# Ranks from block totals, and the ranked pass joined with its neighbours, in a stack of graph layers on one core

## The chip, the cores and the metric

The kernel runs on one core of a Trainium2 chip, with one launch. The metric is device time in microseconds (us). The core has five engines with queues of their own: PE multiplies matrices into PSUM, DVE and ACT do elementwise work and empty PSUM, POOL (GpSimd) does small elementwise work and can issue DMAs, and SP here only issues DMAs. Each engine takes its instructions in the order of the program, and waits on semaphores for what another engine or a DMA has to finish first.

## The reference

A graph with 3327 nodes and 64 features goes through four layers. Each layer normalises x, takes relu, sends it through the dense adjacency matrix and adds the result to x. There are eight products with the matrix, called hops 0 to 7 here: two gated (GRU) hops, one ranked hop, three hops with the squared matrix (weights times mask, both the matrix itself), and two hops of the last layer.

```
h = relu(layernorm(x));  x = x + gru_stack(h, adj)              # hops 0, 1: m = adj @ (x @ W), gates
h = relu(layernorm(x));  support = h @ weight                   # hop 2, the ranked one
mask = (adj != 0); rank = cumsum(mask, axis=1); deg = rank[:, -1:]
k = minimum(deg, 100); pos = rank - (deg - k)
w = mask * where(pos > 0, 0.5 ** (k - pos), 0);  x = x + w @ support + bias
h = relu(layernorm(x));  three times: h = (adj * adj) @ h, h = h @ W.T + b   # hops 3, 4, 5
h = relu(layernorm(x));  two times: h = tanh(concat(adj @ h, h) @ W[k])      # hops 6, 7
```

In the ranked hop the weight of a neighbour is 0.5 to the power of the number of nonzero entries that come after it in the row, where that number is below 100. About 0.5% of the entries are nonzero, and every node is its own neighbour.

## The kernel before

**Tiles.** The nodes are padded to 2 x 13 blocks of 128. The kernel reads the transposed matrix: a source block q (26 of them) is 128 partitions, the target nodes are columns. The targets are cut into four chunks c (`CH`: three of 2 x 384 columns, the last of 2 x 512), and the chunks into two groups: group 0 is chunks 0 and 1, group 1 is chunks 2 and 3. A *tile* is one source block against one group: 768 KB for group 0, 896 KB for group 1, loaded by one DMA from SP into one of 19 slots (`Tile.load`, L281). A *unit* is one hop k, one chunk c and one tile: `propagate` (L376) adds it to the chunk's sum in PSUM, with two halves of 64 output partitions side by side. After its 26 units a chunk's sum is finished, and a task (`after[k]`) makes the next features y[k+1][c] from it: for hops 0 and 1 a GRU cell (`gru`, L527), for hop 1 also a layer norm (L497, with one power on POOL, L510), a row added on POOL (L524) and a split of y into three bf16 terms (`in_three`, L563), since the ranked hop multiplies in bf16.

**Order.** A list `units` is written out by hand: `alone(g, k, ...)` is one hop of one group, and `joint(g, k, ...)` is hops k and k+1 of one group on one load of its tiles. In `joint`, the tiles of the other group's sources come first, each used for hop k and, `LATER` tiles later, for hop k+1; then the tiles of the group's own sources for hop k, then the tiles still waiting, and then the own tiles again for hop k+1, which need hop k's result. `sweep` is the number of last tiles that are taken chunk by chunk, so that the first chunk's task runs beside the second chunk's units. `run` (L450) walks the list: `prepare` loads and masks or squares a tile some units ahead, `expand` makes the operand two units ahead, and `spend` lets the tasks advance step by step as estimated PE time passes. A task whose result is needed at once is finished on the spot (`finish`), so its remaining instructions stand directly before the unit that needs it. The order of instructions on each engine is the order of these calls.

```
    alone(0, 2, descending, sweep=0)
    alone(1, 2, descending, sweep=0)
```

**The ranked hop.** It runs alone for each group, in descending order of source block. `prepare` makes a mask of the tile in half a slot on DVE (L331). `expand` (L338) keeps a running count in PSUM over the whole pass, in two pairs of banks: for each tile it adds `rest` times the mask of the tile before, and `tri` times its own mask (the helper `mm`, L173), so that each entry holds the number of nonzero entries behind it, with its own entry marked. ACT turns the counts into bf16 weights (L365), by writing the exponent bits as int16. Because the counts run on through the pass, the tiles have one fixed order, and PSUM's second half is handed from four `temp` banks to two `pair` tiles for its length (`exchange`, `counting`).

**Other places.** Hops 3 to 5 square the tile, in place where both hops of a `joint` are squared, or into `w4` buffers (`square`, L317: two of three on ACT, one on DVE). Constants are made on POOL and DVE in `more_constants` (L127) while the first tiles load.

Of the kernel before, what the change touches and what calls it, by code (L numbers as in the profile page):

```python
# [37 lines left out]

N, D = 3327, 64
# [13 lines left out]
CAP = 100.0  # L53

# [9 lines left out]
KIND = [PLAIN, PLAIN, RANKED, SQUARED, SQUARED, SQUARED, PLAIN, PLAIN]  # L64
NBUF = 19
PREPARE = {PLAIN: 8, RANKED: 16, SQUARED: 8}
EXPAND = 2
LATER = 4
# [12 lines left out]
def kernel(  # L81
# [13 lines left out]
    work = ctx.enter_context(tc.tile_pool(name="work", bufs=6))  # L95
# [26 lines left out]
    rest = const.tile([P, P], BF16, name="rest")  # L122
    tri = const.tile([P, P], BF16, name="tri")
    bitsb = const.tile([P, 1], F32, name="bitsb")
    bsum = const.tile([P, 2, 2], F32, name="bsum")

    def more_constants():  # L127
# [3 lines left out]
        ones = work.tile([P, P], BF16, name="t2")  # L131
        nc.gpsimd.memset(ones, 1.0)

        nc.gpsimd.affine_select(out=tri, in_=ones, pattern=[[-1, P]], compare_op=ALU.is_gt, fill=0.0,
                                base=0, channel_multiplier=1)
        nc.gpsimd.affine_select(out=tri, in_=tri, pattern=[[-1, P]], compare_op=ALU.not_equal, fill=-128.0,
                                base=0, channel_multiplier=1)
        nc.gpsimd.tensor_tensor(rest, ones, tri, ALU.subtract)
        nc.gpsimd.memset(bitsb, (CAP - 128.0) * TWO7)
# [33 lines left out]
    def mm(out, lhsT, rhs, start=True, stop=True, unchecked=False):  # L173

        for h in range(2):
            hs = slice(h * D, (h + 1) * D)
            nc.tensor.matmul(out[hs], lhsT[:, hs], rhs, start=start, stop=stop, skip_group_check=unchecked)  # L179

# [3 lines left out]
    sum_banks = [psum.tile([P, CWM], F32, name=f"sum{i}") for i in range(4)]  # L184
    counting = []

    def second_half(names, shape):
        pool = tc.tile_pool(name=names, bufs=1, space=bass.MemoryType.PSUM, reuse_waits="tile")
        p = pool.__enter__()
        return pool, [p.tile(shape, F32, name=f"{names}{i}") for i in range(2 if len(shape) > 2 else 4)]  # L190

    half = [second_half("temp", [P, CWM])]

    def exchange(names, shape):
        half[0][0].__exit__(None, None, None)
        half[0] = second_half(names, shape)

    def bank(i):
        return sum_banks[i] if i < 4 else half[0][1][i - 4]

    def take(sums=False):

        pool = idle_sums if sums or counting else idle_temps
        for c in list(tasks):
            if not pool and c not in running:
                advance(c)
        i = pool.popleft()
        return i, bank(i)
# [8 lines left out]
    def features(c):  # L217
        return feat.tile([P, width(c)], F32, name=f"hT{c}")
# [33 lines left out]

    def spend(us):

        for c in list(tasks):
            if c in tasks and c not in running:
                tasks[c][1] -= us
                if tasks[c][1] <= 0:
                    advance(c)
# [8 lines left out]
    class Tile:  # L268

        def __init__(self, q, g, in_place):  # L270
# [3 lines left out]
            self.slot = self.mask = self.before = None  # L274
# [48 lines left out]
    newest = {}  # L323

    def prepare(k, c, t):

        if t.slot is None:
            t.load()
        if KIND[k] == RANKED and t.mask is None:
            t.mask, t.before = Mask(t.w), newest.get(t.g)  # L330
            nc.vector.tensor_scalar(t.mask.view, t.view(), 0.0, None, op0=ALU.not_equal)  # L331
            t.used()
            newest[t.g] = t.mask
        if KIND[k] == SQUARED and t.in_place and c not in t.squares:
            t.squares.add(c)
            square(t.view(c), t.view(c), t.q + c)

    def expand(k, c, t):  # L338

        w = width(c)  # L340
        if KIND[k] == PLAIN or t.in_place:
            return t.view(c)
        wide = work.tile([P, 2, CWM], I16 if KIND[k] == RANKED else F32, name="w4", bufs=4)[:, :, :w]
        if KIND[k] == SQUARED:
            square(wide, t.view(c), t.q + c)
            return wide

        if not counting:
            while len(idle_temps) < 4:
                advance(next(iter(tasks)))
            counting.append(True)
            exchange("pair", [P, 2, CWM])
        a, b = GROUPS[t.g]
        pair = half[0][1][c == b]
        for s in range(2):  # L360
            if t.before is not None:
                mm(pair[:, s, :w], rest, t.before.view[:, s, t.cols(c)], start=False, unchecked=True)
            mm(pair[:, s, :w], tri, t.mask.view[:, s, t.cols(c)], start=t.before is None, unchecked=True)
        spend(STREAM_US * w / CWM)
        nc.scalar.activation(wide, pair[:, :, :w], AF.Relu, bias=bitsb, scale=-TWO7)  # L365
        if c == b:
            if t.before is not None:
                t.before.free()
            if t.q == 0:
                t.mask.free()  # L370
                if t.g == 1:
                    counting.clear()
                    exchange("temp", [P, CWM])
        return wide.bitcast(BF16)

    def propagate(k, c, t, rhs, first, last):  # L376
        w = width(c)
        s, b = divmod(t.q, NB)
        cs = chunk_of(b)
        if y[k][cs] is None:  # L380
            finish(cs)
# [3 lines left out]
        terms = y[k][cs] if KIND[k] == RANKED else [y[k][cs]]  # L385
        for n, yk in enumerate(terms):
            yq = yk[:, b - CH[cs][0], s, :]
            for h in range(2):
                nc.tensor.matmul(acc[h * D:(h + 1) * D, :w], yq, rhs[:, h, :], start=first and n == 0,  # L389
                                 stop=last and n == len(terms) - 1)  # L390
        if KIND[k] != RANKED:
            t.used()
        spend(STREAM_US * w / CWM * (0.75 if KIND[k] == RANKED else 1.0))
        if last:
            begin(c, after[k](c, sums.pop((k, c))))
            if KIND[k] == RANKED and (t.g, c) == (1, NC - 1):
                dead.extend(parts.values())
# [3 lines left out]
    def put(k, c, t):  # L401
        units.append((k, c, t))
        if KIND[k] != RANKED or c == GROUPS[t.g][0]:
            t.uses += 1

    def alone(g, k, order, sweep):
        tiles = [Tile(q, g, KIND[k] == SQUARED) for q in order]
        for t in tiles[:NQ - sweep]:
            for c in GROUPS[g]:
                put(k, c, t)  # L410
        for c in GROUPS[g]:
            for t in tiles[NQ - sweep:]:
                put(k, c, t)

    def joint(g, k, sweep):
        a, b = GROUPS[g]
        in_place = KIND[k] == KIND[k + 1] == SQUARED
        waiting = deque()

        def second():  # L420
            t = waiting.popleft()
            for c in (a, b):
                put(k + 1, c, t)

        for q in sources_of(*GROUPS[1 - g]):
            t = Tile(q, g, in_place)
            for c in (a, b):
                put(k, c, t)
            waiting.append(t)
            if len(waiting) > LATER:  # L430
                second()
        own = [[Tile(q, g, in_place) for q in sources_of(c)] for c in (a, b)]
        both = own[0] + own[1]
        for t in both[:-sweep]:
            for c in (a, b):
                put(k, c, t)
        for c in (a, b):
            for t in both[-sweep:]:
                put(k, c, t)
        while waiting:  # L440
            second()
# [3 lines left out]
        for c in (a, b):  # L445
            for t in own[1]:
                put(k + 1, c, t)

    def run():
        count = {}  # L450
        prepared, expanded = 0, deque()
# [282 lines left out]
```

## Time and profile before

| | us |
|---|---|
| three runs, median (lowest to highest) | 753.68 (751.81 to 754.01) |
| the profiled execution | 751.8 |
| its span | 750.1 |
| PE, ACT, DVE, POOL busy | 717.0, 250.6, 235.7, 42.0 |
| DMA from device memory | 243.64 MB, 326 GB/s over the span |
| PE's clock in all slices | full |

The profile has a page with busy times, with the span in 40 slices (each digit is a busy share in tenths), with the groups of instructions, and with the chain of waits that ended last. The chain is followed back from the last instruction: at each step to what released it. A group's row gives the busy time of its engine, the mean time of one instruction in ns, and the idle time ahead of it with what ended it. Matmuls overlap, so the mean time of one is longer than the time from one to the next.

### The profile page before, as it was taken

The numbers are of one execution on the slowest core, as the hardware profiler recorded it, in microseconds if no ns is written. First come the engines' busy times: TensorE is split into PE (matmuls) and PEld (weight loads), VectorE is DVE, ScalarE is ACT, GpSimd is POOL, SyncE is SP. The second block draws the span as 40 slices with busy tenths as digits, with TensorE's granted clock in tenths as the row PEclk, the third lists the DMA queues.
The fourth block names the chain that finished last, engine by engine and source line by source line (L and its number), as shares of the span: only waits on it lengthen the run. The fifth ranks groups of instructions, "written<-read, shape, count | busy, mean of one in ns | idle before, by whom it ended". The sixth has DMA issues, their size and how long they took to land.

```text
span 750.1 us, 12253 instructions
## 1 busy us (share of the span) xinstructions
PE 717.0 (96%) x5240; PEld 345.7 (46%) x5240; DVE 235.7 (31%) x346; ACT 250.6 (33%) x314; POOL 42.0 (6%) x38
## 2 busy tenths in 40 slices
PE   3978999999998999999999999999999999999997
PEld 2423433434456666666334444334444454344444
DVE  6101201326369347431944213430252610000000
ACT  1101001111046777778947422740054501000000
POOL 5100000001102003000300000000020000000000
PEclk9999999999999999999999999999999999999999
DMA  9999994679999999995999949972999299906991
GB/s 294 401 401 406 405 405 187 240 266 404 401 402 400 404 405 384 386 370 201 407 401 400 403 144 398 405 291 77 379 361 313 74 369 405 366 28 229 398 403 68
DMA packets 79174, 245.29 MB, mean 327 GB/s; under 512 B 4880, under 2 KB 5520, under 8 KB 79120
## 3 DMA queue, kind: packets, MB, share of 16 engines
q1 hardware_dynamic: 78240, 243.55, 85.1%
q10 hardware_dynamic: 880, 0.96, 0.5%
q8 instruction: 41, 0.67, 0.4%
q14 instruction: 13, 0.11, 0.0%
HBM read 243.64 MB, written 0.85 MB: 326 GB/s over the span
## 4 chain that ended last, share of the span: by engine, by line
PE 83%; DMA 8%; DVE 5%; SPq 1%; issue 1%; POOL 1%; ACT 1%; ACTq 0%; DVEq 0%; POOLq 0%
PE sum L389 66%; PE pair L179 9%; PE temp L179 8%; DMA adj<-in_adjT 7%; SPq L284 1%; PE sum L179 1%; DMA brow<-in_bias_rows 1%; DVE adj L331 1%; POOL st L510 1%; DVE t L504 1%; DVE st L502 0%; DVE xs L518 0%; DVE adj L321 0%; DVE st L508 0%; DVE t L507 0%
## 5 line engine op out<-in xcount | busy, mean ns | idle before, releaser
L389 PE MATMUL sum<-adj,y 128*64 128x384 f32 (+1 forms) x2704 | 489.8, 516 | 21.7 <-DMA adj<-in_adjT 19.7
L389 PEld LDWEIGHTS sum<-adj,y 128*64 128x64 f32 x2704 | 192.4, 137 | 289.9 <-issue 249.1
L365 ACT ACTIVATE w<-pair,bitsb 128x768 int16<-128x768 f32 x104 | 98.8, 954 | 33.1 <-PE pair L179 30.1
L319 ACT ACTIVATE adj<-adj 128x768 f32<-128x768 f32 (+1 forms) x103 | 86.1, 906 | 30.8 <-DMA adj<-in_adjT 28.6
L467 DVE COPY t<-sum 128x384 f32<-128x384 f32 x16 | 8.9, 558 | 275.0 <-PE sum L389 275.0
L389 PE MATMUL sum<-w,adj 128*64 128x384 bf16 (+1 forms) x624 | 72.9, 340 | 3.4 <-ACT adj L575 2.2
L179 PE MATMUL pair<-adj,tri 128*64 128x384 bf16 (+1 forms) x416 | 70.8, 339 | 0.0
L179 PE MATMUL pair<-adj,rest 128*64 128x384 bf16 (+1 forms) x400 | 68.7, 339 | 0.6 <-ACT w L365 0.4
L331 DVE TENSOR_SCALAR adj<-adj 128x1536 bf16<-128x1536 f32 (+1 forms) x52 | 53.1, 1028 | 51.2 <-PE pair L179 38.6
L321 DVE TENSOR_TENSOR adj<-adj 128x768 f32<-128x768 f32 (+1 forms) x53 | 53.9, 1063 | 46.8 <-DMA adj<-in_adjT 46.8
L510 POOL TENSOR_TENSOR st<-st,mhalf 128x6 f32<-128x6 f32 (+1 forms) x16 | 27.4, 1752 | 560.9 <-DVE st L509 560.9
L538 ACT ACTIVATE w<-temp,bsum 128x384 f32<-128x384 f32 (+1 forms) x14 | 8.6, 611 | 138.8 <-PE temp L179 138.8
L389 PEld LDWEIGHTS <-adj 128*64 128x64 bf16 x624 | 36.8, 110 | 22.0 <-ACT adj L575 2.8
L389 PE MATMUL sum<-w,y 128*64 128x384 f32 x208 | 36.4, 487 | 0.8 <-DVE w L321 0.8
L319 ACT ACTIVATE w<-adj 128x768 f32<-128x768 f32 x35 | 27.5, 838 | 16.0 <-PE sum L389 9.5
L465 ACT COPY t<-sum 128x384 f32<-128x384 f32 (+1 forms) x16 | 8.5, 532 | 71.9 <-PE sum L389 71.9
L179 PEld LDWEIGHTS <-tri 128*64 128x64 bf16 x416 | 24.6, 110 | 12.5 <-issue 1.1
L179 PEld LDWEIGHTS <-rest 128*64 128x64 bf16 x400 | 24.0, 110 | 13.1 <-issue 1.6
L493 ACT COPY hT<-temp 128x384 f32<-128x384 f32 (+1 forms) x12 | 6.1, 506 | 62.7 <-PE temp L179 62.7
L179 PE MATMUL temp<-bd,t 128*64 128x128 f32 (+1 forms) x296 | 24.3, 279 | 0.4 <-ACT t L465 0.4
L321 DVE TENSOR_TENSOR w<-adj 128x768 f32<-128x768 f32 x17 | 16.0, 956 | 25.9 <-PE sum L389 19.7
L389 PEld LDWEIGHTS sum<-w,y 128*64 128x64 f32 x208 | 14.5, 137 | 18.7 <-issue 14.8
(74 smaller groups left out, 273.0 us busy)
## 6 DMA issues: line engine op xcount, KB each, us to landing
adj<-in_adjT SPq DMA_DIRECT2D x156, 768.0 KB, 11.9
adj<-in_adjT SPq DMA_DIRECT2D x130, 896.0 KB, 9.7
adj<-in_weights SPq DMA_DIRECT2D x2, 352.0 KB, 7.1
xs<-in_x SPq DMA_DIRECT2D x1, 640.0 KB, 5.0
out<-xs ACTq DMA_DIRECT2D x3, 192.0 KB, 1.9
out<-xs ACTq DMA_DIRECT2D x1, 256.0 KB, 6.0
xs<-in_x SPq DMA_DIRECT2D x1, 192.0 KB, 2.4
brow<-in_bias_rows ACTq DMA_DIRECT2D x1, 96.0 KB, 6.9
```

Source lines behind the costliest of these rows:

```text
L179: nc.tensor.matmul(out[hs], lhsT[:, hs], rhs, start=start, stop=stop, skip_group_check=unchecked)
L284: nc.sync.dma_start(out=slots[self.slot][:, :, :self.w], in_=adjT[self.q * P:(self.q + 1) * P, :].rearrange("p (s w) -> p s w", s=2)[:, :, ...
L319: nc.scalar.activation(sq, v, AF.Square)
L321: nc.vector.tensor_tensor(sq, v, v, ALU.mult)
L331: nc.vector.tensor_scalar(t.mask.view, t.view(), 0.0, None, op0=ALU.not_equal)
L365: nc.scalar.activation(wide, pair[:, :, :w], AF.Relu, bias=bitsb, scale=-TWO7)
L389: nc.tensor.matmul(acc[h * D:(h + 1) * D, :w], yq, rhs[:, h, :], start=first and n == 0, stop=last and n == len(terms) - 1)
L465: nc.scalar.copy(m, acc[1][:, :width(c)])
L467: nc.vector.tensor_copy(m, acc[1][:, :width(c)])
L504: nc.vector.tensor_tensor(xc[:, :n], v, st[:, 1, :n, None].to_broadcast([P, n, D]), ALU.subtract)
L510: nc.gpsimd.tensor_tensor(st[:, 3, :n], st[:, 2, :n], mhalf[:, :n], ALU.pow)
L538: nc.scalar.activation(gate, ps[:, :w], AF.Sigmoid, bias=bsum[:, cell, g:g + 1])
```

## The change

The counts behind each tile no longer come from a running sum in the ranked hop. They are taken in hop 0, where the same tiles pass anyway. For every tile a mask is made there too (unit kind `COUNT`), and four short matmuls with a block of ones and zeros (`behind`) add its column sums to the totals of all source blocks that come before it. When hop 0 of a group is done, `totals` holds, for each source block and column, the number of nonzero entries in all blocks behind it.

In the ranked hop a tile's mask gets only 127 rows from DVE. The last row is filled from `totals`, by two DMAs from POOL's queue, and `tri` has a row for it, so one product with `tri` gives the whole count and no tile depends on another. The 26 real last rows (`lastw`) are handled as one more unit per chunk (`SPECIAL`): `mask_last` loads them by two DMAs from SP for each group, and `lasty` collects the matching rows of y[2] by twelve small DMAs from POOL for each chunk, at the end of `in_three`. The count is emptied from four single banks again, one half by ACT and the other by DVE.

As the order is free, the ranked hop is joined: hops 1 and 2 of group 0 share their tiles, and hops 2 and 3 of group 1. In `joint`, waiting tiles are now taken two at a time while the own tiles pass. Loads have a look-ahead of their own (`LOAD`, `RESERVE`). The built program has 234 tile loads instead of 286, 208 `behind` matmuls in place of 400 `rest` matmuls, and 152 DMAs on POOL instead of none.

```diff
-PREPARE = {PLAIN: 8, RANKED: 16, SQUARED: 8}
-LATER = 4
+LOAD = 16
+PREPARE = {COUNT: 6, PLAIN: 6, RANKED: 12, SQUARED: 6}
+RESERVE = 3
...
-        nc.gpsimd.tensor_tensor(rest, ones, tri, ALU.subtract)
+        nc.gpsimd.memset(tri[:, P - 1:P], 0.0)
+        nc.gpsimd.memset(bitsb, BITS)
+        nc.gpsimd.memset(lasty, 0.0)
...
     def prepare(k, c, t):
...
+            rows = P - 1 if kind == RANKED else P
+            nc.vector.tensor_scalar(t.mask.view[:rows], t.view()[:rows], 0.0, None, op0=ALU.not_equal)
             t.used()
-            newest[t.g] = t.mask
+            if kind == RANKED:
+
+                for ch in GROUPS[t.g]:
+                    finish(("count", ch))
+                for s in range(2):
+                    nc.gpsimd.dma_start(out=t.mask.view[P - 1:P, s, :],
+                                        in_=totals[t.g][s * D + t.q:s * D + t.q + 1, :])
...
     def expand(k, c, t):
...
         for s in range(2):
-            if t.before is not None:
-                mm(pair[:, s, :w], rest, t.before.view[:, s, t.cols(c)], start=False, unchecked=True)
-            mm(pair[:, s, :w], tri, t.mask.view[:, s, t.cols(c)], start=t.before is None, unchecked=True)
-        spend(STREAM_US * w / CWM)
-        nc.scalar.activation(wide, pair[:, :, :w], AF.Relu, bias=bitsb, scale=-TWO7)
+            i, ps = take()
+            mm(ps[:, :w], tri, t.mask.view[:, s, t.cols(c)])
+            if s:
+                nc.vector.tensor_scalar(wide[:, s], ps[:, :w], BITS, 0.0, op0=ALU.add, op1=ALU.max)
+            else:
+                nc.scalar.activation(wide[:, s], ps[:, :w], AF.Relu, bias=bitsb)
+            give(i)
...
+    def count(t, first, last):
+        for c in GROUPS[t.g]:
+            w = width(c)
+            if first:
+                counts[c] = take()
+            for s in range(2):
+                nc.tensor.matmul(counts[c][1][s * D:(s + 1) * D, :w], behind[:, NQ - 1 - t.q:NQ - 1 - t.q + D],
+                                 t.mask.view[:, s, t.cols(c)], start=first, stop=last)
...
+    def mask_last(g):
...
+        nc.gpsimd.memset(v, 0.0)
+        rows = adjT.rearrange("(q p) (s n) -> q p s n", p=P, s=2)
+        for s in range(2):
+            nc.sync.dma_start(out=v[s * D:s * D + NQ], in_=rows[:, P - 1, s, w0:w0 + w])
+        yield 12.0
+        nc.vector.tensor_scalar(v, v, 0.0, 129.0 * TWO7, op0=ALU.not_equal, op1=ALU.mult)
...
     def propagate(k, c, t, rhs, first, last):
...
+        if t is SPECIAL:
+            for ch in range(NC):
+                if ch != c:
+                    finish(ch)
+            terms = [[lasty[:, h, i, :] for h in range(2)] for i in range(3)]
+            rhs = [rhs, rhs]
...
     def in_three(h, c):
...
+        yield 1.5
+        b0, b1 = CH[c]
+        for s in range(2):
+            for h in range(2):
+                for i in range(3):
+                    q = h * D + s * NB
+                    nc.gpsimd.dma_start(out=lasty[q + b0:q + b1, h, i, :], in_=terms[i][P - 1:P, :, s, :])
...
-    alone(0, 0, ascending, sweep=2)
-    joint(1, 0, sweep=3)
-    alone(0, 1, ascending, sweep=6)
-    alone(0, 2, descending, sweep=0)
-    alone(1, 2, descending, sweep=0)
-    alone(1, 3, ascending, sweep=6)
-    joint(0, 3, sweep=8)
+    alone(0, 0, sweep=2, lag=5)
+    joint(1, 0, sweep=3, later=4, lag=2)
+    joint(0, 1, sweep=6, later=10)
+    joint(1, 2, sweep=6, later=5)
+    joint(0, 3, sweep=8, later=4)
...
     begin(NC, more_constants())
+    begin(NC + 1, mask_last(0))
+    begin(NC + 2, later_task(60.0, mask_last(1)))
     run()
```

## The prediction

> **What bounds the kernel now.** I read the page first (shares, slices, groups), then the chain of waits in order of time, then the timelines of POOL and SP in the first 36 us.
>
> The page, head, slices and six groups:
>
> ```profile
> PE 717.0 (96%) x5240; PEld 345.7 (46%) x5240; DVE 235.7 (31%) x346; ACT 250.6 (33%) x314; POOL 42.0 (6%) x38
> ...
> DMA  9999994679999999995999949972999299906991
> ...
> L389 PE MATMUL sum<-adj,y 128*64 128x384 f32 (+1 forms) x2704 | 489.8, 516 | 21.7 <-DMA adj<-in_adjT 19.7
> L365 ACT ACTIVATE w<-pair,bitsb 128x768 int16<-128x768 f32 x104 | 98.8, 954 | 33.1 <-PE pair L179 30.1
> L179 PE MATMUL pair<-adj,rest 128*64 128x384 bf16 (+1 forms) x400 | 68.7, 339 | 0.6 <-ACT w L365 0.4
> L331 DVE TENSOR_SCALAR adj<-adj 128x1536 bf16<-128x1536 f32 (+1 forms) x52 | 53.1, 1028 | 51.2 <-PE pair L179 38.6
> L510 POOL TENSOR_TENSOR st<-st,mhalf 128x6 f32<-128x6 f32 (+1 forms) x16 | 27.4, 1752 | 560.9 <-DVE st L509 560.9
> adj<-in_adjT SPq DMA_DIRECT2D x156, 768.0 KB, 11.9
> ```
>
> PE is the bound, and POOL is nearly empty. Durations of matmuls overlap, so rates come from the chain of waits (start, us, what):
>
> ```profile
> 47.43 14.85 DMA adj<-in_adjT
> 62.32 2.16 PE sum L389 x12
> 64.48 3.87 PE temp L179 x24
> ...
> 250.02 0.65 PE pair L179 x8
> ...
> 251.16 0.65 PE pair L179 x8
> ...
> 397.06 41.28 PE sum L389 x256
> ```
>
> A 384-column f32 matmul instruction costs 41.28/256 = 0.161 us (four a unit: 0.645). A ranked unit of 384 columns costs 251.16 - 250.02 = 1.14: eight pair matmuls at 0.081 (0.65) and six rank matmuls (0.49). For 512 columns the chain has 0.86 for eight, 0.107 each. Until 62.3 the end is set by loads: the PE timeline at 54 to 60 us has a tile every 1.95 us with 0.45 us of waiting in it.
>
> POOL and SP at the start (start, us, engine):
>
> ```profile
> 16.23 1.64 POOL L510 TENSOR_TENSOR st<-st,mhalf 128x8 f32<-128x8 f32 x1 [2.20 <-DVE st L509]
> 17.82 0.20 POOL L132 MEMSET t<- 128x128 bf16 x1
> ...
> 20.68 0.20 POOL L141 MEMSET t<- 128x128 f32 x1
> ```
>
> ```profile
> 2.97 34.22 SPq L284 DMA_DIRECT2D adj<-in_adjT  x20
> ```
>
> SP issues the first tile at 2.97; PE gets it at 12.39.
>
> **What the Trainium skill says.** "DMA: Bandwidth & Descriptors", section "Latency and other measured facts": a DMA issued from GpSimd has about 1 us to the first byte, put down to its descriptors being emitted in software; section "Anatomy of one DMA — SWDGE (gpsimd) path" adds a fixed 2 us to completion, and says that DMA engines do not wait on semaphores, the issuing sequencer does. The last agrees with the trace: SP's own waits list 344.6 us for PE. No run here shows a DMA from POOL. "SBUF — State Buffer", section "SBUF: two separate sides": a DVE instruction in a two-port mode keeps GpSimd from writing descriptors. The masks are such instructions by their rate (958 ns for 1536 elements, while the two-input square takes 984 for 768).
>
> **The change, part by part** (against the span, 750.1).
>
> *PE work.* The 400 `rest` matmuls go: 300 x 0.081 + 100 x 0.107 = 35.0. The counts add 208 matmuls, 0.32 us a tile of group 0 and 0.37 of group 1. In the first pass 21 of 26 fit in the 0.45 us of waiting per tile; five follow the last tile (1.6), and group 1 pays 9.8 in full. SPECIAL adds three units of 0.49 and one of 0.65: 2.1. Net -21.5.
>
> *Loads.* 286 tile loads become 234, since hops 1 and 2 of group 0, and 2 and 3 of group 1, share tiles. That pays only where PE waits: PE is idle 12.8 us after 62.3 (windows: 687.7 minus 674.9 busy), at the load-bound hop 1 (chain at 196 to 206), the starts of the ranked passes and at 347 to 368. I take -10.
>
> *The start.* `mask_last(0)` runs before the schedule, so its two small loads stand ahead of all tiles in SP's order, and the first waits for a POOL memset that stands behind all four L510 and the constants. L510 ends at 17.87; the constants without `rest` and with two small memsets end near 20.3; the 128x768 memset is 2.44 (128x2816, L111) x 768/2816 = 0.67. So SP goes on at 21.0, two issues of 0.6, and the first tile is issued at 22.3 instead of 2.97. Behind the waiting instruction stand all tiles, and PE behind them. Some of these 19.3 us come back, since x and weights are long in: I take the shortest landing of a tile in the trace, 4.5 us, instead of the first one's 9.4. First tile at 26.8 instead of 12.4; this stage is paced by loads, so nothing hides it: +14.4.
>
> *The joined order.* In hop 1 with pass 2 of group 0, the last tiles are its own, and the built program's PE order has the first ranked matmul of tile 0 directly behind them. It needs y[2] of chunk 0. From the end of that sum: L467 0.56, gates 3.87, L546, L547, L551 1.78, L553 to L557 2.03, transposes 0.65, L518 0.56, L502 to L509 2.62, L510 1.65, L513 and L514 0.73, in_three 2.13: 16.6, with some 20 hand-overs 18.5. PE meanwhile has the other chunk's six units (3.9), gates 3.9, tri 1.0, transposes 0.7: 9.4. Wait 9. Chunk 1's gates stand behind that; its y[2] costs 4 more. +13. In hop 0 to 1 of group 1 the loop drains the waiting tiles before the end, so the cover is three units and two counts: +2. Before, four waiting tiles (6 us) lay there.
>
> *POOL's queue.* 104 row DMAs (two a mask) and 48 for `lasty` (twelve a chunk), all in POOL's order with L510 and L524. A row also waits until PE has left that half of the slot; behind it waits L510, and DVE's L514 for that. Price unknown in the trace: 0.3 us if generation overlaps, 1.4 if masks lock it out; I take the skill's 1 us, and 2 to complete.
> (a) In that pass PE reaches the first ranked unit at about 22 us (22 units of hop 1 at 0.645, and some 8 of gates). The third mask is wanted four ranked units of 0.81 and two of 0.645 later, at 26.5. Twelve DMAs for chunk 2, possible from about 15 us, go ahead of its rows, which wait for PE at 22, then for the queue at 27: done at 31, wait 4.5. Twelve for chunk 3, gated by DVE's evictions, start at 33; they end at 45, two more rows and completion make 49. PE is there 4.5 after 31, at 35.5: wait 13.5. Sum 18.
> (b) After y[2] of chunk 0 (18.5): L524 1.1, 12 for its `lasty`, 12 rows, and only then chunk 1's L510, at 43.6. y[2] of chunk 1 comes at 48.7 where PE is ready at 32.7: 16 instead of 4. Then its own twelve, to 60.7 and 2; PE reaches SPECIAL at 53.6: 9. Sum 21 over the part above.
> (c) Pass 2 with hop 3 of group 1: 2 us of POOL against 3.4 of PE a tile, except in the rank-only stretch of own tiles: +3.
> Together +42.
>
> *Hidden.* Evictions split between ACT and DVE: per ranked tile of group 0 DVE does 0.96 + 2 x 0.56 = 2.1, PE 1.6 to 2.9. With squares in group 1: 1.10 + 1.25 + 0.73 = 3.1 against 3.4. Covered by PE unless DVE is held up; without cover some 10. Buffers (hT one instead of two, t2 five): readers finish long before, 0.
>
> Sum: -21.5 - 10 + 14.4 + 13 + 2 + 42 = +40, span 790. What lies around it is 751.8 - 750.1 = 1.7. The profiled execution, 751.8, is 1.9 under the median of the three runs (753.68), so 793 beside that; I round down to 790, as PE may get to the lasty bursts with some rows already in.
>
> **Rivals.**
> 1. *POOL is not felt* (0.3 us a DMA or less): -21.5 - 10 + 14.4 + 15 = -2 and nothing for POOL: span 748, time 750 (752 beside the median), 0.3% faster. For: POOL is 94% free; the DMAs are tiny. Against: bursts of twelve stand directly ahead of rows and of L510. It decides below about 0.35 us, where POOL's 42 shrink to some 2.
> 2. *Half price* (0.6 us): (a) 10, (b) 8, (c) 2: 20 in place of 42, so 768.
> 3. *Masks and descriptors block each other, or DVE becomes the bound* of the joined passes (1.4 us a DMA, or the uncovered 10 and more): (a) 29, (b) 35, 42 becoming 69, so 817.
> 4. *The start costs nothing* because SP's wait is met earlier: 776. The POOL order speaks against it.
> That loads drop is certain from the built program.
>
> **How the numbers follow.** Forecast 0.58 (own range 775 to 808), rival 1 0.11, rival 2 0.13, rival 3 0.14, rival 4 0.04. Below 752 lies 0.1, above 822 another 0.08: range 752 to 822. The measurement tells 0.3% from no change. Faster by over that takes most of rival 1: 0.08; within it 0.03; slower 0.89.
>
> **What would show it.** First tile matmul at 26 to 27 us and PE in the first pass ending near 77; a POOL row of 104 and 48 DMA issues near 1 us; waits of PE for POOL's DMAs (tri matmuls on mask rows, SPECIAL on lasty) of 25 to 50 us in hop 1 with pass 2; one L510 late by 10 us or more there; hops 3 to 7 unchanged in length. PE after the first pass short of waits would make the forecast wrong, as would a first tile at 13 us.

## The result: 8.3% slower

| | before | after |
|---|---|---|
| median of the runs (lowest to highest), us | 753.0 (751.81 to 754.01) | 815.71 (813.21 to 818.48) |
| span of the profiled execution, us | 750.1 | 811.4 |
| TensorE's mean clock in it | 1.000 | 0.978 |

The ratio is 1.0834, with a 95% interval of 1.0792 to 1.0876. The forecast was 790 with a range of 752 to 822: the direction and the range held, the likeliest value was 26 us too low. Single terms of its sum were wrong by up to 30 us, in opposite directions.

The page of the kernel after, with the lines that answer to those shown of before:

```profile
PE 721.9 (89%) x5072; PEld 355.5 (44%) x5072; DVE 343.0 (42%) x508; ACT 217.2 (27%) x322; POOL 134.2 (17%) x196
...
PEclk9999999999989969999999999999999999999999
DMA  3899969449127437336647996999167899981992
...
L464 PE MATMUL sum<-adj,y 128*64 128x384 f32 (+1 forms) x2912 | 541.4, 517 | 35.6 <-DMA adj<-in_adjT 28.2
...
L339 DVE TENSOR_SCALAR adj<-adj 128x1536 bf16<-128x1536 f32 (+3 forms) x104 | 103.6, 1021 | 48.0 <-PE temp L399 47.8
...
L380 ACT ACTIVATE e<-temp,bitsb 128x384 int16<-128x384 f32 (+1 forms) x104 | 63.2, 607 | 89.1 <-PE temp L198 75.6
...
L198 PE MATMUL temp<-adj,tri 128*64 128x384 bf16 (+1 forms) x416 | 65.7, 352 | 20.3 <-DMA adj<-totals 10.9
L378 DVE TENSOR_SCALAR e<-temp 128x384 int16<-128x384 f32 (+1 forms) x104 | 59.7, 586 | 45.3 <-PE temp L198 33.8
L346 POOL DMA_DIRECT2D adj<-totals x104 | 62.5, 607 | 37.4 <-PE temp L198 27.8
```

PE does 168 matmuls fewer and is busy 4.9 us longer. DVE makes 104 masks (L339) where it made 52. PE's clock row, all nines before, now has an 8 and a 6. The eviction of the counts is split over two rows (L380 on ACT, L378 on DVE), and a POOL transfer of a row (L346) occupies its queue for 0.607 us. DMA is light in the middle of the span, where it stood at 9 before: the tiles are shared, as the change says, and PE still waits. For whom, the waits of PE over the whole span tell (us in total, times, longest):

```profile
PE sum L464 <- DMA adj<-in_adjT: 28.2, 3, 27.2
PE sum L464 <- ACT adj L701: 12.9, 4, 7.0
PE temp L198 <- DMA adj<-totals: 10.9, 6, 5.9
PE sum L464 <- DVE e L378: 7.5, 9, 1.7
PE temp L198 <- DVE e L378: 6.3, 10, 2.4
PE temp L198 <- DVE hT L683: 5.8, 3, 2.8
PE sum L464 <- DVE y L642: 3.3, 1, 3.3
```

The first row is for tiles: 27.2 is the wait for the first tile, and 1.0 are two later ones. Before, the same row came to 19.7, of which the first tile was 12.4. The rest lay between 14 and 62.4 us, all of it in the first pass:

```profile
PE sum L389 <- DMA adj<-in_adjT: 7.3, 15, 1.1
```

The full lists of waits before and after account for all but 1.1 us of the difference of the spans, 61.3 us. PE's idle time went from 33.1 (750.1 minus 717.0) to 89.5, which is 56.4 more; its busy time is the other 4.9.

| where PE's time went | before | after | difference | forecast |
|---|---|---|---|---|
| waits for adjacency tiles: the first | 12.4 | 27.2 | +14.8 | +14.4 |
| the same, later tiles, all in the first pass | 7.3 | 1.0 | -6.3 | -6.7 (counts put into these pauses) |
| the same, after the first pass, where loads are now shared | 0 | 0 | 0 | -10 |
| the way to y[2]: hT, then the three terms (L683 in hop 1, L701) | 2.2 | 15.7 | +13.5 | +13 |
| hop 0 to 1 of the second group (L683, L729) | 1.3 | 3.7 | +2.4 | +2 |
| POOL's transfers (rows, last ranks) | 0 | 11.6 | +11.6 | +42 |
| evictions, masks and y on DVE's order (L378, L339, L642; before L365, on ACT, and L514) | 2.0 | 21.3 | +19.3 | 0 |
| other waits | | | +1.1 | |
| PE busy | 717.0 | 721.9 | +4.9 | -14.8 (the forecast's -21.5 is this with the 6.7 above) |

The start is as forecast. The timelines of POOL and of SP in the first 70 us (start, us, engine). POOL:

```profile
20.81 0.74 POOL L430 MEMSET adj<- 128x768 f32 x1
```

SP:

```profile
21.57 0.77 SPq L433 DMA_DIRECT2D adj<-in_adjT  x2
22.39 47.60 SPq L292 DMA_DIRECT2D adj<-in_adjT  x29
```

SP's two small transfers (L433) stand ahead of all tiles and wait for POOL's clearing of 20.81 to 21.55, so the first tile is issued at 22.39 instead of 2.97.

In the chain of waits (start, us, what) the long run of f32 units has the rate it had:

```profile
455.50 46.44 PE sum L464 x288
```

46.44/288 is 0.161 us a matmul, as before, so the units themselves did not change; the power on POOL (L638) is the same too, 27.4 us in 16.

The rest happens in two stretches. I cut the span where ACT begins to copy the sum of a group's second chunk out of PSUM. The first joined stretch runs from the end of hop 1 of group 1 to the end of hop 2 of group 0 (before: 167.9 to 283.6; after: 198.3 to 341.0), the second from there to the end of hop 3 of group 1. The windows of the two kernels (window, us, busy us and instructions of PE, PEld, DVE, ACT, POOL, then PE's clock, DMA share, GB/s), before:

```profile
167.90:283.60 115.70, 111.07 (x1076) 66.64 (x1074) 67.12 (x99) 58.52 (x73) 11.49 (x8) 1.00 1.03 403
283.60:394.90 111.30, 109.67 (x974) 60.10 (x972) 57.95 (x74) 83.78 (x91) 12.25 (x8) 1.00 0.94 358
```

and after:

```profile
198.30:341.00 142.70, 109.11 (x886) 69.38 (x883) 90.28 (x154) 41.95 (x74) 75.01 (x117) 0.89 0.47 162
341.00:453.40 112.40, 97.37 (x785) 55.62 (x785) 87.90 (x122) 63.80 (x92) 38.44 (x52) 0.98 0.56 190
```

The first stretch became 27 us longer, with less PE work in it, half the traffic and a third more of DVE. The second did not become shorter, although 189 matmuls went out of it: PE is busy 12 us less and waits 13 us more.

What one wait looks like, from PE's timeline after (start, us, engine line operation, and in brackets the idle time before it and who ended it):

```profile
231.28 1.09 PE L198 MATMUL temp<-adj,tri 128*64 128x384 bf16 x4 [5.91 <-DMA adj<-totals]
```

and further on, where the first y[2] is wanted:

```profile
294.20 0.53 PE L464 MATMUL sum<-e,adj 128*64 128x384 bf16 x2 [6.98 <-ACT adj L701]
```

The windows behind these two waits (columns as above):

```profile
231.28:236.76 5.48, 5.46 (x29) 2.96 (x30) 3.45 (x5) 1.16 (x2) 4.29 (x8) 0.55 0.03 3
294.20:301.25 7.05, 6.38 (x24) 2.34 (x26) 1.96 (x3) 1.09 (x2) 6.26 (x11) 0.51 0.41 129
```

At 231.28 a product with `tri` had waited 5.91 us for a row of totals. At 294.20 the first unit with y[2] had waited 6.98. In both places PE's clock behind the wait is near half, 0.55 and 0.51, for 5 to 7 us. So a wait costs more than its own length.

Why the row was late is in POOL's timeline (same columns):

```profile
221.32 7.13 POOL L712 DMA_DIRECT2D lasty<-adj  x12
```

Twelve transfers for `lasty` hold POOL for 7.13 us ahead of the next rows. The y[2] of 294.20 was little held up by other work. Its way begins with the copy of the sum on DVE:

```profile
274.87 0.56 DVE L595 COPY t<-sum 128x384 f32<-128x384 f32 x1 [6.01 <-PE sum L464]
```

From there to 294.20 are 19.3 us, and 21.0 to the last of the three terms, where the forecast had 18.5. Five masks stand on DVE behind the copy (275.34 to 279.76), but PE makes the gates in that time: the last products start at 278.41 and 279.05, and the step that takes them (L672) starts at 279.69, so the masks cost it at most some 0.6 us. The tanh after it (L677, 282.93) stands behind two evictions on ACT and loses some 2 us. What is new is that PE runs out of work long before the way is done.

Waits for evictions do come from DVE's order. The longest of them, on PE:

```profile
312.26 0.35 PE L198 MATMUL temp<-adj,tri 128*64 128x384 bf16 x2 [2.37 <-DVE e L378]
```

and what stands ahead of that eviction (L378, at 311.65) on DVE:

```profile
308.75 0.54 DVE L679 TENSOR_TENSOR gates<-hT,gates 128x384 f32<-128x384 f32 x1
...
310.79 0.95 DVE L339 TENSOR_SCALAR adj<-adj 127x1536 bf16<-127x1536 f32 x1
311.65 0.55 DVE L378 TENSOR_SCALAR e<-temp 128x384 int16<-128x384 f32 x1
```

PE has no work from 309.9 on. The eviction that it needs stands behind four steps of the other chunk's GRU and a mask, 2.9 us in all.

### The profile page after: what moved, and what is told of

The parts are those of the page before. It is cut to its first block, busy times and chain, and to the rows that moved or that the text cites. A ratio compares the mean times of both kernels' runs of the same rounds, so it can differ in the third digit from the quotient of the medians.

```text
span 811.4 us, 12297 instructions
## 1 busy us (share of the span) xinstructions
PE 721.9 (89%) x5072; PEld 355.5 (44%) x5072; DVE 343.0 (42%) x508; ACT 217.2 (27%) x322; POOL 134.2 (17%) x196
## 3 DMA queue, kind: packets, MB, share of 16 engines
HBM read 199.68 MB, written 0.85 MB: 247 GB/s over the span
## 5 line engine op out<-in xcount | busy, mean ns | idle before, releaser
L464 PE MATMUL sum<-adj,y 128*64 128x384 f32 (+1 forms) x2912 | 541.4, 517 | 35.6 <-DMA adj<-in_adjT 28.2
L339 DVE TENSOR_SCALAR adj<-adj 128x1536 bf16<-128x1536 f32 (+3 forms) x104 | 103.6, 1021 | 48.0 <-PE temp L399 47.8
L327 ACT ACTIVATE adj<-adj 128x768 f32<-128x768 f32 (+1 forms) x138 | 112.3, 885 | 41.9 <-PE sum L464 23.5
L464 PE MATMUL sum<-e,adj 128*64 128x384 bf16 (+1 forms) x624 | 76.3, 349 | 20.5 <-ACT adj L701 12.9
L638 POOL TENSOR_TENSOR st<-st,mhalf 128x6 f32<-128x6 f32 (+1 forms) x16 | 27.4, 1713 | 405.9 <-DVE st L637 405.9
L380 ACT ACTIVATE e<-temp,bitsb 128x384 int16<-128x384 f32 (+1 forms) x104 | 63.2, 607 | 89.1 <-PE temp L198 75.6
L198 PE MATMUL temp<-adj,tri 128*64 128x384 bf16 (+1 forms) x416 | 65.7, 352 | 20.3 <-DMA adj<-totals 10.9
L378 DVE TENSOR_SCALAR e<-temp 128x384 int16<-128x384 f32 (+1 forms) x104 | 59.7, 586 | 45.3 <-PE temp L198 33.8
L346 POOL DMA_DIRECT2D adj<-totals x104 | 62.5, 607 | 37.4 <-PE temp L198 27.8
L464 PEld LDWEIGHTS <-adj 128*64 128x64 bf16 x624 | 44.2, 112 | 42.7 <-issue 16.5
L712 POOL DMA_DIRECT2D lasty<-adj x48 | 28.1, 592 | 6.4 <-ACT adj L701 4.0
L399 PE MATMUL temp<-adj,behind 128*64 128x384 bf16 x208 | 26.2, 339 | 0.0
L198 PEld LDWEIGHTS temp<-bd,t 128*64 128x64 f32 x320 | 19.3, 138 | 8.9 <-issue 4.1
```

The costliest lines, as they stand in the source:

```text
L327: nc.scalar.activation(sq, v, AF.Square)
L339: nc.vector.tensor_scalar(t.mask.view[:rows], t.view()[:rows], 0.0, None, op0=ALU.not_equal)
L346: nc.gpsimd.dma_start(out=t.mask.view[P - 1:P, s, :], in_=totals[t.g][s * D + t.q:s * D + t.q + 1, :])
L378: nc.vector.tensor_scalar(wide[:, s], ps[:, :w], BITS, 0.0, op0=ALU.add, op1=ALU.max)
L380: nc.scalar.activation(wide[:, s], ps[:, :w], AF.Relu, bias=bitsb)
L399: nc.tensor.matmul(counts[c][1][s * D:(s + 1) * D, :w], behind[:, NQ - 1 - t.q:NQ - 1 - t.q + D], t.mask.view[:, s, t.cols(c)], start=firs ...
```

## The experiments

The theory was: the early stall at the start, POOL's queue at 0.6 us a transfer, and DVE's order on the way to y[2] and to the evictions, each wait made longer by a halved clock behind it. The rivals were: one of these causes alone, with the others without effect. Each kernel is the kernel after with the edit that is shown. Differences are of medians, against 815.7 unless another kernel is named; the runs of the kernel after spread over 5 us, so a difference is good to some 3 us (the kernel before had a median of 753.4 to 754.1 beside the experiments). The stretches are those of the section above.

| kernel | median, us | ratio to before (95%) | up to the end of hop 1, group 1 | first stretch | second stretch | rest |
|---|---|---|---|---|---|---|
| before | 753 | | 167.9 | 115.7 | 111.3 | 355.2 |
| after | 815.7 | 1.0834 (1.0792 to 1.0876) | 198.3 | 142.7 | 112.4 | 358.0 |
| fetch delayed | 804.4 | 1.0667 (1.0640 to 1.0695) | 186.9 | 144.5 | 114.2 | 359.2 |
| no `lasty` transfers | 805.5 | 1.0684 (1.0665 to 1.0703) | 201.0 | 131.7 | 114.2 | 358.0 |
| no row transfers | 798.5 | 1.0589 (1.0567 to 1.0610) | 198.2 | 130.0 | 110.0 | 358.1 |
| neither | 799.4 | 1.0601 (1.0584 to 1.0619) | 201.3 | 128.6 | 110.2 | 357.5 |
| fewer transfers | 808.8 | 1.0744 (1.0717 to 1.0772) | 199.5 | 135.3 | 112.7 | 358.0 |
| five tiles kept back | 811.1 | 1.0789 (1.0750 to 1.0828) | 200.3 | 137.2 | 112.2 | 358.1 |
| no counts | 792.9 | 1.0518 (1.0491 to 1.0545) | 175.7 | 144.0 | 114.2 | 357.8 |
| no squares | 809.4 | 1.0733 (1.0702 to 1.0765) | 201.1 | 142.6 | 108.6 | 355.9 |
| squares on ACT | 809.5 | 1.0747 (1.0728 to 1.0765) | 200.0 | 142.0 | 108.6 | 357.2 |
| join undone | 796.2 | 1.0577 (1.0554 to 1.0601) | 199.7 | 127.9 | 108.3 | 357.8 |
| join undone, fetch delayed, fewer transfers | 767.0 | 1.0185 (1.0159 to 1.0211) | 186.0 | 113.4 | 107.8 | 357.8 |
| the same, evictions balanced | 760.8 | 1.0099 (1.0068 to 1.0130) | 187.5 | 111.1 | 103.5 | 357.8 |

### The start

```diff
-    begin(NC + 1, mask_last(0))
+    begin(NC + 1, later_task(20.0, mask_last(0)))
```

> The one edit: the fetch of the rows of the 128th ranks for the first group (POOL's clearing, two transfers on SP's queue, DVE's pass) is put behind a delay of 20 us in the planner instead of ahead of the first adjacency tile. Theory (the load queue's first tile is held up by the wait for POOL's clearing, and nothing later makes up for it): -14 us against the changed kernel, 799 to 804 us. Rival (the early stall only moves waits that would come later anyway, since the loads are ahead of TensorE by the end of pass 0): -5 us or less, 810 us or more.

Measured: 804.4, so -11.3. The theory's size was -14, but it is far from the rival's -5. The two small transfers now stand at 36 us in SP's order, the first tile is issued at 2.99, and the gain of 11.4 at the end of hop 1 of group 1 (186.9 against 198.3) is kept nearly whole: loads were ahead of PE later, but an early stall of PE was not made up for.

### POOL's transfers

`lasty` left out:

```diff
         yield 1.5
-        b0, b1 = CH[c]
-        for s in range(2):
-            for h in range(2):
...
```

> The 48 POOL transfers that gather the last ranks' vectors (lasty) are left out, so the last ranks' term of hop 2 is zero. Theory (POOL's queue at 0.6 us a transfer holds up the row transfers queued behind these bursts, and a wait also halves TensorE's clock for some us): -6 to -12 us against the changed kernel, the waits of the mask matmuls for a row of totals gone from the stretch of hop 1. Rival A (VectorE's order alone sets hop 1's waits): -2 to 0. Rival B (POOL at the forecast's 1 us a transfer): -20 or more.

The rows left out:

```diff
-            rows = P - 1 if kind == RANKED else P
+            rows = P
...
-                for s in range(2):
-                    nc.gpsimd.dma_start(out=t.mask.view[P - 1:P, s, :],
...
```

> The 104 POOL transfers of a row of totals into each mask are left out and VectorE writes all 128 rows of the mask, so that row 128 carries the edge of its own rank in place of the total. Theory (POOL's queue at 0.6 us, with the halved clock after each wait): -8 to -14 us; TensorE then waits nowhere for a row. Rival A (VectorE's order sets hop 1's and hop 2's waits): -3 to 0. Rival B (POOL at 1 us a transfer): -30 or more.

Both left out, the two edits together:

> Both are left out, the 48 and the 104 POOL transfers, so that the kernel computes neither the totals' row nor the last ranks' term. Theory: -12 to -20 us against the changed kernel, less than the sum of the two single ones since they hold up the same queue; the stretch of hop 2's second group (from the end of hop 2's first group, some 114 us) stays within 4 us of what it is, because there VectorE's order and not POOL sets the waits. Rival A (VectorE's order everywhere): -4 to 0. Rival B (POOL's queue is the whole of what the joined passes lost, in hop 2's second group too): -40 or more.

Measured: -10.2, -17.2 and -16.3. The first is within the theory's range; the waits for rows fell with it from 10.9 to 4.5, and in the first stretch from 9.6 to 3.0, so they did not vanish there as the theory had it. The rows cost 17.2, somewhat more than its 14. Both together give no more than the rows alone, which fits that `lasty` costs what it does by holding up rows. Of the 12 to 14 us that the first stretch gains, the waits for rows are 9.6; the rest fits the halved clock, 0.89 in that stretch after and 0.92 without the transfers, but is not separated from it. The second stretch stays within 2.2 us of what it was, so another cause holds it. The waits of PE without any of these transfers:

```profile
PE sum L461 <- ACT adj L698: 12.9, 4, 7.0
```

The wait for y[2] (L698 here) is what it was to the tenth, and the waits for evictions, 14.4 in the same list, are no shorter than 13.8. So the forecast's part (b), in which POOL makes y[2] later still, did not happen.

The same data in fewer instructions:

```diff
-                for s in range(2):
-                    nc.gpsimd.dma_start(out=t.mask.view[P - 1:P, s, :],
-                                        in_=totals[t.g][s * D + t.q:s * D + t.q + 1, :])
+                nc.gpsimd.dma_start(out=t.mask.view[P - 1:P, :, :],
+                                    in_=totals[t.g][t.q:t.q + D + 1:D, :])
...
-                for i in range(3):
...
+                q = h * D + s * NB
+                nc.gpsimd.dma_start(out=lasty[q + b0:q + b1, h].rearrange("p i d -> p (i d)"),
+                                    in_=room[P - 1:P, :, s].rearrange("p b i d -> p b (i d)"))
```

> The same transfers in fewer instructions on POOL: both halves of a mask's row of totals in one (104 become 52), the three terms of a last rank's vector in one (48 become 16, with the terms laid side by side in the slot). Theory (the queue's length on POOL is the cost, 16.3 us for 152 transfers): -7 to -11 us against the changed kernel. Rival (the 2 to 3.6 us until a transfer has landed is the cost): -3 or less.

Measured: -6.9, just short of the theory's range and well beyond the rival's. 68 transfers cost 9.4 us where 152 cost 16.3. A row's transfer also landed sooner, 2.6 to 2.7 us after its issue instead of 3.4 to 3.6, so the run does not separate the queue from the landing cleanly.

### The order around y[2]

```diff
             both(t)
-            second(2)
+            second(2 if KIND[k + 1] != RANKED else max(0, min(2, len(waiting) - 5)))
```

> In the joint pass of hop 1 and hop 2 of the first group, five waiting tiles of hop 2 are kept back behind the last units of hop 1 instead of none, so that TensorE has ten ranked units of about 0.8 us (8 us) while y[2] of the first chunk is made. Theory (the serial way to y[2] leaves TensorE idle there, with a halved clock behind each wait): -7 to -12 us against the changed kernel, hop 2 of the first group ending that much sooner. Rival (VectorE's masks and evictions bound that stretch, whatever the order): -2 or less.

Measured: -4.6, between the two. The wait for y[2] fell from 12.9 to 5.6, so the cover does what the theory says. But later waits took over: in the first stretch the waits for rows rose from 9.6 to 13.5 and those of `tri` for evictions from 3.7 to 5.3. That is one wait taken over in part by the next.

### The counts

```diff
...
-    alone(0, 0, sweep=2, lag=5)
-    joint(1, 0, sweep=3, later=4, lag=2)
+    alone(0, 0, sweep=2)
+    joint(1, 0, sweep=3, later=4)
...
-    begin(NC + 1, mask_last(0))
-    begin(NC + 2, later_task(60.0, mask_last(1)))
+    for g in range(2):
+        nc.gpsimd.memset(totals[g], 0.0)
+        nc.gpsimd.memset(lastw[g], 0)
```

> The counts of hop 0 are left out with their masks and the rows of the 128th ranks; totals and the last ranks' weights are set to zero instead, all transfers stay. The early fetch falls away too, so it is compared with the run that delays this fetch (804.4 us). Theory (208 matmuls on TensorE, 11.4 us of the forecast's sum, some of it hidden in the load-bound first pass): -10 to -14 us against that run, 790 to 794. Rival (the 52 masks more on VectorE cost as well): -18 or more.

Measured: 792.9, which is -11.5 against the kernel with the delayed fetch, all of it before the first joined stretch (175.7 against 186.9). The forecast had 18.1 us of matmuls, 6.7 of them in the pauses of the first pass, and so 11.4. The pauses are indeed back in this run: the waits for later tiles are 7.2 instead of 2.4. Nothing is left over for the 52 masks on DVE.

### DVE in the second stretch

Squares left out (`square` returns at once and the tile itself is the operand), and, in the diff, squares all on ACT:

```diff
     def square(sq, v, turn):
-        if turn % 3:
+        if True:
             nc.scalar.activation(sq, v, AF.Square)
```

> All squares of the weights are left out (hops 3 to 7 use the weights as they are). Theory (in hop 2 with hop 3 of the second group masks, evictions and squares stand in one order on VectorE and ScalarE, and TensorE waits for an eviction behind a mask or a square): that stretch, 112.4 us from the end of hop 2 of the first group to the end of hop 3 of the second, comes to 102 to 106, the whole to -6 to -12 us against the changed kernel. Rival (the waits there come from the serial way between hops and from late loads): stretch 110 or more, whole -3 or less.

> All squares on ScalarE instead of two thirds of them; same outputs. Theory (VectorE's order holds up evictions): the same stretch -3 to -7 us, as VectorE loses 21 us of squares there. Rival (ScalarE's order is as full, 87 us of work in 112): 0, or +2 to +5.

Measured: the second stretch is 108.6 in both, 3.8 less, and the whole -6.3 and -6.2, of which the spread of the kernel after may be a part. So the squares on DVE do stand in the way, by some 4 us, and ACT has room for them. The theory had put more on them (102 to 106). Most of what is left stands on DVE too. PE's waits in the second stretch, with squares on ACT, are 3.7 for evictions, 2.6 for y (L642), 2.4 for masks and 2.2 for rows; 4.0 and 2.6 were for evictions and 3.3 for y before this edit.

### The join undone

```diff
...
-    joint(0, 1, sweep=6, later=10)
-    joint(1, 2, sweep=6, later=5)
+    alone(0, 1, sweep=6)
+    alone(0, 2, sweep=0)
+    alone(1, 2, sweep=0)
+    alone(1, 3, sweep=6)
```

> The joined order alone is undone: hops 1 and 2 of the first group and hops 2 and 3 of the second run one after the other, each with its own loads as before the change; the counts, the rows of totals and the last ranks' term stay. Hop 2 of the first group takes the other group's tiles first, so that some 26 ranked units (20 us) stand between the end of hop 1 and the first use of y[2] of the first group. Theory (the join left y[2] without cover, with TensorE's clock halved behind each wait, and crowded VectorE): the stretch from the end of hop 1 of the second group to the end of hop 2 of the first comes from 142.7 to 112 to 120 us, the next one from 112.4 to 102 to 108, the whole to -26 to -40 us against the changed kernel. Rival (the 52 loads more and POOL's queue hold a ranked pass of its own just as much): -12 or less.

Measured: 796.2, -19.6. That lies between what the two expected, and the two stretches, 127.9 and 108.3, are just outside the theory's ranges. 52 loads come back (243.98 MB are read instead of 199.68), and the kernel is faster. PE's waits:

```profile
PE temp L198 <- DVE e L378: 17.2, 14, 4.2
PE temp L198 <- DMA adj<-totals: 10.9, 4, 5.9
```

No wait for y[2] is left, and still only 1.0 for tiles after the first. The rows' waits stayed at 10.9 and the evictions' waits rose: both are in the ranked pass itself, joined or not, as the rival said.

With the delayed fetch and the fewer transfers added:

> The join undone, the early fetch delayed by 20 us, and the fewer transfers, together. Theory (the three are separate costs, with some overlap between join and transfers): 757 to 772 us, still not under the kernel before, because the counts' 11.5 us remain and passes of their own are near the rate of their loads. Rival (they are one cost, and TensorE's saved work comes through once the stalls are gone): 735 to 750.

Measured: 767.0, inside the theory's range. The three edits save 48.7 together and 37.8 one by one (11.3, 19.6 and 6.9). The rows' waits are down to 1.1 here, from 10.9 with the join undone alone: with fewer transfers and the passes apart, POOL's queue hardly holds PE up. The windows of the two stretches:

```profile
186.00:299.40 113.40, 101.57 (x888) 61.43 (x886) 88.43 (x151) 41.58 (x74) 43.96 (x56) 0.97 1.01 388
299.40:407.20 107.80, 97.70 (x786) 53.69 (x784) 87.05 (x126) 64.39 (x90) 27.27 (x28) 0.98 1.02 395
```

They are 2.3 and 3.5 us shorter than before the change, with 21.5 us less of PE busy time (199.3 against 220.8), and DMA's share is full in both (1.01 and 1.02), as it was before in the first. A full share does not make the loads the limit, though: in both stretches neither PE nor a mask waits for a tile (squares do, 2.6 us on DVE and ACT together), and PE waits 16.5 us for evictions on DVE.

The last edit on top of it:

```diff
-            if s:
+            if s and t.q % 2:
                 nc.vector.tensor_scalar(wide[:, s], ps[:, :w], BITS, 0.0, op0=ALU.add, op1=ALU.max)
```

> The kernel of the three edits together (join undone, fetch delayed, fewer transfers; 767.0 us), with one edit more: for every second source tile ScalarE makes both evictions of the expansion, so that VectorE loses 26 of its 52 evictions in each ranked pass, about 15 us of 64.6 in a stretch of 68.5, and ScalarE gains as much on 33.9. Theory (VectorE's order, 94% full in that stretch, is what is left of the loss): the 16 us of waits for its evictions shrink below 6, 753 to 760 us. Rival (the loads, whose DMA share is 1.00 there, set the length of the pass): the waits move to the tiles or the masks, 763 to 768. Second rival (ScalarE's two evictions in a row are a longer way for a unit than one on each engine): 770 or more.

Measured: 760.8, -6.2, just outside the theory's 753 to 760 and under the rival's 763. The time came down as the theory says, but what should show it did not come: the waits for DVE's evictions fell only from 16.5 to 13.5, although DVE's load in the stretch of 68.5 us fell from 94% (64.6) to 79% (54.3). The loads are not what is left: they are the same as ahead of this edit, both stretches became shorter (111.1 and 103.5), and again neither PE nor a mask waits for a tile. What is left is the place in DVE's order. Of the 13.5, 8.2 lie in the first of the two ranked passes, all between 243 and 271 us, where DVE makes y[2] as well. The longest wait there, 3.57, ends at 247.06; its eviction stands behind a layer norm step, four GRU steps and a mask on DVE, 243.07 to 246.46. Another, 2.80, ends at 263.28 behind a mask that took 2.61 us instead of 0.95; why it did is open.

No version was under the kernel before. The best one is still 7.8 us behind. It loses 19.6 ahead of the first joined stretch (187.5 against 167.9), of which the counts are 11.5, and 2.6 behind the second, and gains 12.4 in the two.

## Why the forecast was right, and where not

**Right.** The start (14.8 of waiting where 14.4 was worked out), the way to y[2] (13.5 and 13), hop 0 to 1 (2.4 and 2) and the counts (11.5 and 11.4) came as the forecast's steps had them, and so did the number of loads and the 6.7 us of counts in the pauses of the first pass (these pauses shrank by 6.3). A POOL transfer's landing, 2.1 to 3.6 us from issue, lies somewhat above the fixed 2 us to completion that the Trainium skill states ("DMA: Bandwidth & Descriptors", section "Anatomy of one DMA — SWDGE (gpsimd) path"). Of the signs that the forecast named, the first tile (27.2) and the hops behind the second stretch (358.0 against 355.2) came. Waits of 25 to 50 us for POOL's transfers and a power on POOL 10 us late did not come.

**The step "POOL's queue" was too large.** It took 1 us a transfer and made 42 us; the row of the page has 0.607, and all transfers together cost 16.3 by experiment. The 1 us that it took is quoted there as a time to the first byte, and that is not the time for which a transfer occupies the queue. The price was that of rival 2, whose 20 is near, though 8 of it is a part (b) that did not come. The mechanism (bursts for `lasty` ahead of rows) was right in part (a). Part (b), y[2] late because a power on POOL stands behind transfers, was wrong: PE waited as long for y[2] without a transfer. The masks did not lock POOL out to the 1.4 us a transfer of rival 3: 0.607 is the mean over all 104 rows.

**The step "Hidden" failed, by 19 us of waits.** It compared sums: 2.1 us of DVE a tile against 1.6 to 2.9 of PE. But an eviction is needed within two units, and DVE works in order, so a mask of 0.95 us, a square, or a stretch of a GRU or layer norm in front of it is a wait even where DVE's mean load is far from full: it is 63% in the first stretch (90.28 of 142.7) and 78% in the second. In the second stretch the waits, most of them of this kind, ate the whole gain of 12 us of PE work. Moving work off DVE took back 6.2 us twice, with the squares and with the evictions, and the traces show the order at single waits; that the order is behind all of the 19 is read from the list of waits. The forecast had "without cover some 10"; it came to twice that. Rival 3's other half, DVE as the bound, is nearest to that, but DVE was not full, and its 817, near the result, was worked out from longer waits for POOL: that is luck.

**The clock was not in the sum.** The matmul work adds up to -35.0 + 18.1 + 2.1 = -14.8 (18.1 is the counts with those in the pauses), and busy time rose by 4.9: 19.7 more. A clock of 0.978 over 811.4 us is at most 17.9 of it. So most of the difference can be slower work after waits, and not more work. The Trainium skill has this ("TensorE: Matmul & The Clock Gate", section "Part 1: The HAM clock gate"): the array falls to half its rate after an idle window of about 3.4 us and is back after one that is busy. The trace agrees for waits of 5.91 and 6.98, with 5 to 7 us near half rate after them; a shorter one of 2.61 had it too in one execution (last section). The forecast did not use it. In the trace of before PE has only one wait that long, for the first tile; the eight matmuls behind it take 2.83 us, eight later ones 1.46, though the clock is given as full there.

**The step "Loads" failed: -10 was forecast, and at most 1.3 came.** It took PE's idle time after 62.3, 12.8 us, and the chain of waits as a sign that PE waits for tiles there. But PE's own list has no wait for a tile after the first pass. The load in the chain at 196 to 206 (9.44 us) held up a mask on DVE, and PE waited 1.3 us behind that (L467). The 6.3 us by which the waits for later tiles fell belong to the counts: with the join undone and all 286 loads back, they stay at 1.0, and without the counts they are 7.2. The join took away y[2]'s cover; undoing it is 19.6 us faster.

**The net.** POOL was 30 us of waits too high in the forecast. DVE's order was 19 too low, PE's busy time 20 and the loads 10. So 790 was near by luck, as errors cancelled, and a reader who trusts its terms one by one would have mended the wrong part first.

## What to carry to other kernels

In an in-order engine ask how long the one instruction that PE waits for may stand behind others, not whether the engine's sum fits under PE's. Before loads are shared to save time, look in PE's own list whether it waits for tiles in that pass; a full DMA share, or a load in the chain of waits, does not say so. And sharing them must not take the units that covered a serial step between passes. Price a new wait of PE like those of 6 to 7 us here at its length plus some 3 us; that is an estimate from the 5 to 7 us near half rate behind them.

## What the runs showed of the hardware

Whether the clock halves after a short wait differs from execution to execution. At the end of hop 0 of group 1 the wait for hT is 2.61 us in the kernel after and in the one without POOL's transfers, with the same program up to there. PE's timeline after:

```profile
165.43 0.88 PE L198 MATMUL temp<-ident,hT 128*64 128x128 f32 x12 [2.61 <-DVE hT L683]
```

and without the transfers:

```profile
165.41 1.40 PE L198 MATMUL temp<-ident,hT 128*64 128x128 f32 x12 [2.61 <-DVE hT L680]
```

The same twelve matmuls take 1.40 instead of 0.88 us in the second, and the end of hop 1 of group 1 comes 3.0 us later (201.3 against 198.3). So a wait shorter than the window that the Trainium skill gives was followed by a halved clock here, and a difference of 3 us between single profiled executions says little here.

A small transfer occupied POOL for 0.607 us, and for 0.712 where it has two source rows instead of one, so that the rows took 36.9 us of POOL instead of 62.5. With the join undone the two were 0.655 and 0.762.
